# Spreading the attention's second scores over the partitions: a DRAM scratch in place of TensorE's transposes

## The chip, the cores and the metric

The kernel runs on one core of one Trainium2 chip, in float32 throughout. The metric is the device time of one execution in microseconds. Before the change it is 2218.47 us, the median of three runs (2218.12 to 2219.33).

The engines are named as in the profile: PE is TensorE's matmuls and PEld its weight loads, DVE is VectorE, ACT is ScalarE, POOL is GpSimd, and SP is SyncE, which here only issues DMAs.

## The reference

The input x has 128 graphs of 128 nodes with 512 features; `adj` is one 128 x 128 weighted adjacency matrix. Four graph layers follow each other, each added to its input and normalised over the features. What matters here is layer 2, a graph attention:

```python
h  = jnp.einsum('bnc,cf->bnf', x, W)
s1 = jnp.einsum('bnf,f->bn', h, a1)
s2 = jnp.einsum('bnf,f->bn', h, a2)
e = jax.nn.leaky_relu(s1[:, :, None] + s2[:, None, :], negative_slope=ALPHA)
e = e * mask[None, :, :]            # mask is adj
att = jax.nn.softmax(e, axis=2)
h_prime = jnp.einsum('bij,bjf->bif', att, h)
return jax.nn.elu(h_prime + beta * h)
```

For every graph, `e[i, j]` is a sum of a score of node i and a score of node j. With node i on the partitions, `s1` is one number per partition, while `s2` has to lie along the free dimension, the same row on all 128 partitions. The scores, however, come out with the node on the partitions, both of them. Turning `s2` from a column into a row on every partition is the "spread".

## The kernel before, in words

The 128 graphs go through in 32 groups of four (`G = 4`, `NG = 32`). All pieces of work of all layers and groups are put in one list, each with a due time, and the list is sorted by these times at the end (lines 817 to 827). `TABLE` (line 231) has the due times of one group, in slots of 2.48 us by the source's own constant; group g's are shifted by 28 g. So in one period of 28 slots TensorE works on layer 0 of group g+2, layer 1 of group g+1 and layers 2 and 3 of groups g and g-1, interleaved. The first two groups and the last three have due times of their own (`FIRST`, `LAST`). `InOrder` (line 18) keeps each engine's instructions, and SyncE's DMAs, in the order in which they are issued: an engine that waits holds up everything behind it on that engine. The semaphores are put in by the framework, from what each instruction reads and writes.

The names that matter:

- The large products (`product`, line 339: `y` of layer 0, `m` and `v` of layer 1, `z` of layer 2) use seven block products instead of eight (Strassen's scheme in Winograd's form). GpSimd makes the sums of the left factors (`left_factors`, line 294: tiles `s_y`, `yT` and the like). TensorE takes seven steps in the order 1, 2, 6, 5, 7, 3, 4, each of eight matmuls of 256 columns, into PSUM regions `r...`. After each step ScalarE or VectorE reads the region out (`out`, line 359). Steps 6, 7 and 4 add onto the region of step 1, so each of them has to wait until the step before it on that region has been read. For y the read is VectorE's `x<-r_y,x`, which adds to x in place.
- `scale_dots` (line 580) finishes the scores of a group on VectorE: a tile `d12`, kept as `s12[g]`, of 128 partitions x (s1, s2) x 4 graphs. Its last instruction is `d<-d,rstd`.
- `spread` (line 623) turns `s2` with four 128 x 128 transposes on TensorE, against the identity, into one PSUM bank `p_s2`, printed as `p_s` in the profile. Banks come from a ring of three (`bank`, line 82).
- `leaky` (line 632) is VectorE's `e<-p_s,d`, which adds the two scores for four graphs at once, and `e<-e`, the leaky ReLU. After it come `weighted` (GpSimd times `adj`), `greatest` (VectorE, `nm`), `exps` (ScalarE), `divide` (VectorE's `rs`, GpSimd's product), `turn_att` (four transposes, `p_eT`), and `gather`.
- SyncE's queue holds, in one period: the 16 moves of `xT` for g+1, four stores, the load of x for g+3 (1 MB, due 64 in g's slots), and the 16 moves of `relT` for g+1.

Of the kernel before, what the change touches and what calls it, by code (L numbers as in the profile page):

```python
# [8 lines left out]
FP = mybir.dt.float32  # L9
# [20 lines left out]
def kernel(  # L30
# [33 lines left out]
    pe, dve, act, pool = (InOrder(tc, e) for e in (nc.tensor, nc.vector, nc.scalar, nc.gpsimd))  # L64
    sync = InOrder(tc, nc.sync)
    B, N, D = x.shape
    P = 128
# [4 lines left out]
    G = 4  # L72
    NG = B // G
# [4 lines left out]
    work = ctx.enter_context(tc.tile_pool(name="work", bufs=1))  # L78
    small = ctx.enter_context(tc.tile_pool(name="small", bufs=4))
    psum = ctx.enter_context(tc.tile_pool(name="psum", bufs=1, space=bass.MemoryType.PSUM))  # L80

    def bank(name):
        return psum.tile([P, D], FP, tag="ps", name=name, bufs=3)
# [40 lines left out]
    ident = const.tile([P, P], FP)  # L124
# [102 lines left out]
    def row(at, step, n=G):  # L227
        return [at + i * step for i in range(n)]
# [8 lines left out]
        move_rel=row(41.2, 0.1), inverse=[42.5], v=row(42, 1, 7), attend=row(50.6, 1),  # L237
        residual=row(51.0, 1), dots=[51.7, 53.8, 54.9, 55.6], norm1=[54.6], scale=[57.2],
        apply1=row(65.4, 0.33),
        spread=[61.6], leaky=[62.0], weighted=[63.4], greatest=[64.3], exps=[64.4],  # L240
        divide=[65.8], turn_att=[68.6], with_beta=[69.0], gather=row(71.5, 1),
        z_sums=row(75.3, 0.5), z_w=row(77, 1, 7), exp=[87.5, 88.5, 90.4, 92.0],
        elu=[87.8, 89.4, 92.8, 93.8], norm2=[95.0], apply2=row(95.7, 0.33),
# [14 lines left out]
            greatest=[10.5], exps=[11.2], divide=[13.6], turn_att=[18.3], with_beta=[18.9],  # L258
# [11 lines left out]
            greatest=[52.4], exps=row(53.2, 0.6), divide=row(53.9, 0.6),  # L270
# [344 lines left out]
    s12 = {}  # L615
# [3 lines left out]

    def layer2(g, t):  # L620
        s = {}

        def spread():
            s["p"] = bank(f"p_s2_{g}")
            for b in range(G):
                pe.transpose(
                    s["p"][:, b * P : (b + 1) * P],
                    s12[g][:, 1, b : b + 1].to_broadcast([P, P]),
                    ident,
                )  # L630

        def leaky():
            e = work.tile([P, G, P], FP, tag="e", name=f"e_{g}")
            dve.tensor_tensor(
                e,
                s["p"].rearrange("p (b n) -> p b n", b=G),
                s12[g][:, 0, :, None].to_broadcast([P, G, P]),
                ALU.add,
            )
            dve.scalar_tensor_tensor(e, e, ALPHA, e, op0=ALU.mult, op1=ALU.max)  # L640
            s["e"] = e
# [89 lines left out]

        n = G // len(t["exps"])
        emit(t["spread"][0], spread)
        emit(t["leaky"][0], leaky)
        emit(t["weighted"][0], weighted)
        emit(t["greatest"][0], greatest)
# [86 lines left out]
    for g in range(NG):  # L823
        for layer in (layer0, layer1, layer2, layer3):
            layer(g, times(g))
# [31 lines left out]
```

## Time and profile before

| From the page | before |
|---|---|
| time of the runs, median | 2218.47 us |
| profiled span | 2214.6 us |
| PE busy | 2170.9 us, 98% |
| PEld busy | 1839.6 us, 83% |
| DVE busy | 1547.9 us, 70% |
| ACT busy | 1102.5 us, 50% |
| POOL busy | 907.7 us, 41% |
| DMA | 115.15 MB, mean 52 GB/s |

A line of a group in the profile gives the source line, the engine, the operation, "tile written <- tiles read", the shapes, the count, and then times. Since all operations go through one helper, every line number is L26, and one reads by tile names. Buffer numbers and group numbers are left out of the names. A timeline line gives the start and the length in us, and in brackets the idle time of that engine ahead of it with what ended it. Matmuls are pipelined: the length of a line of PE reaches to the modelled end of its last matmul, so the cost of a stretch is read from the start of one line to the start of the next.

A busy engine of 98% isn't proof that only this engine counts. Whether a change elsewhere reaches it is read from how long before the wait's end the other engines had been done.

### The profile page before, as it was taken

What the parts mean: (1) busy time and instruction counts of PE and PEld (TensorE: products, weight loads), DVE (VectorE), ACT (ScalarE), POOL (GpSimd) and SP (SyncE); (2) the same over time, 40 slices, a digit from 0 to 9 for tenths busy, and PEclk for the clock granted to TensorE, in tenths of its full rate; (3) what the DMA queues carried; (4) which work ended last, traced back from release to release, by engine and by line L of the source; (5) the groups of instructions that cost most, each with busy time, mean ns of one, the idle gap of its engine ahead of it and who ended that gap; (6) DMA issues with size and microseconds to landing.
All of it is one profiled execution on the core that took longest, in us unless ns stands there. A gap on an engine that the chain in (4) does not pass through costs nothing.

```text
span 2214.6 us, 31863 instructions
## 1 busy us (share of the span) xinstructions
PE 2170.9 (98%) x11073; PEld 1839.6 (83%) x11073; DVE 1547.9 (70%) x3290; ACT 1102.5 (50%) x2446; POOL 907.7 (41%) x743
## 2 busy tenths in 40 slices
PE   7999999999999999999999999999999999999996
PEld 5788888888888888888888888888888888888873
DVE  4657766767766767776767776767767677667676
ACT  2224445554445554445554445554455554455547
POOL 3334444334444344443344443344443344443321
PEclk9999999999999999999999999999999999999998
DMA  4011222211222211222112222112222112221101
GB/s 167 25 20 29 61 60 62 62 20 49 60 60 63 58 21 52 59 61 62 44 31 56 58 62 63 41 30 59 58 62 63 29 39 62 59 63 44 21 28 57
DMA packets 333295, 115.15 MB, mean 52 GB/s; under 512 B 297424, under 2 KB 297552, under 8 KB 333136
## 3 DMA queue, kind: packets, MB, share of 16 engines
q1 hardware_dynamic: 331936, 110.77, 19.7%
q10 hardware_dynamic: 1200, 2.36, 0.3%
q8 instruction: 88, 1.44, 0.3%
q14 instruction: 71, 0.58, 0.1%
HBM read 39.65 MB, written 33.55 MB: 33 GB/s over the span
## 4 chain that ended last, share of the span: by engine, by line
PE 93%; DVE 3%; ACT 2%; POOL 1%; issue 1%; DMA 0%; ACTq 0%; DVEq 0%; POOLq 0%
PE r_y L26 17%; PE r_v L26 17%; PE r_m L26 17%; PE r_z L26 17%; PE p_z L26 5%; PE p_rel L26 5%; PE p_y L26 5%; PE p_o L26 5%; PE p_a L26 5%; DVE x L26 1%; ACT x L26 1%; DVE st L26 1%; PE p_eT L26 1%; PE p_m L26 1%; PE p_s L26 1%
## 5 line engine op out<-in xcount | busy, mean ns | idle before, releaser
L26 ACT ACTIVATE x<-x,nmean,rstd 128x512 f32<-128x512 f32 x384 | 288.6, 808 | 120.8 <-DVE nmean L26 120.8
L26 DVE BATCH_NORM_STATS2 st<-x 128x6 f32<-128x512 f32 x384 | 263.8, 687 | 8.8
L26 POOL TENSOR_TENSOR x<-x,bias_sb 128x512 f32<-128x512 f32 x128 | 170.1, 1331 | 137.9 <-PE p_y L26 137.5
L26 DVE SCALAR_TENSOR_TENSOR x<-m,x 128x512 f32<-128x512 f32 x128 | 114.4, 894 | 108.5 <-ACT m L26 98.5
L26 POOL TENSOR_TENSOR s_x<-xT 128x512 f32<-128x512 f32 x64 | 82.2, 1285 | 261.1 <-DMA xT<-xB 250.2
L26 ACT COPY c<-r_z 128x512 f32<-128x512 f32 x124 | 71.2, 574 | 223.3 <-PE r_z L26 198.0
L26 ACT COPY yT<-p_y 128x512 f32<-128x512 f32 x128 | 75.1, 586 | 213.6 <-PE p_y L26 213.6
L26 POOL TENSOR_TENSOR rstd<-ve,mhalf 128x4 f32<-128x4 f32 (+1 forms) x99 | 98.5, 995 | 194.1 <-DVE ve L26 188.9
L26 DVE TENSOR_TENSOR x<-r_y,x 128x512 f32<-128x512 f32 x224 | 151.7, 678 | 31.2 <-PE r_y L26 31.0
L26 DVE SCALAR_TENSOR_TENSOR scr<-x,wa 128x512 f32<-128x512 f32 x256 | 161.5, 675 | 0.0
L26 DVE STREAM_TRANSPOSE xB<-x 128x512 f32<-128x512 f32 x120 | 81.2, 696 | 108.7 <-ACT x L26 97.7
L26 PEld LDWEIGHTS p_y<-adjT,x 128*128 128x128 f32 x1024 | 136.9, 196 | 11.2 <-ACT adjT L26 4.8
L26 POOL TENSOR_TENSOR s_z<-zT 128x512 f32<-128x512 f32 x31 | 39.4, 1270 | 255.9 <-ACT zT L26 255.9
L26 PE MATMUL p_y<-adjT,x 128*128 128x128 f32 x1024 | 137.6, 280 | 4.5 <-ACT adjT L26 4.5
L26 PEld LDWEIGHTS p_z<-eT,x 128*128 128x128 f32 x1024 | 134.0, 192 | 7.9 <-issue 1.0
L26 PEld LDWEIGHTS p_rel<-xT,tT 128*128 128x128 f32 x1024 | 134.1, 191 | 7.4 <-DVE tT L26 0.8
L26 DVE TENSOR_REDUCE mx<-p_a 128x1 f32<-128x512 f32 x128 | 88.3, 691 | 69.6 <-PE p_a L26 69.6
L26 PE MATMUL p_a<-x,adjT 128*128 128x512 f32 x256 | 130.8, 596 | 5.8 <-DVE mx L26 4.4
L26 ACT COPY tT<-r_m 128x512 f32<-128x512 f32 x128 | 75.6, 590 | 121.6 <-PE r_m L26 121.6
L26 PE MATMUL p_rel<-xT,tT 128*128 128x128 f32 x1024 | 134.9, 275 | 0.6 <-DVE tT L26 0.6
L26 PE MATMUL p_z<-eT,x 128*128 128x128 f32 x1024 | 134.7, 275 | 0.1
L26 PE MATMUL p_o<-v,relT 128*128 128x512 f32 x256 | 130.4, 593 | 0.3 <-ACT v L26 0.3
(129 smaller groups left out, 5268.6 us busy)
## 6 DMA issues: line engine op xcount, KB each, us to landing
out_dram<-x SPq DMA_DIRECT2D x128, 256.0 KB, 2.5
x<-in_x_dram SPq DMA_DIRECT2D x31, 1024.0 KB, 5.3
xT<-xB SPq DMA_DIRECT2D x480, 64.0 KB, 2.3
relT<-relB SPq DMA_DIRECT2D x512, 16.0 KB, 1.8
w_sb<-in_L_gnn_weight_dram ACTq DMA_DIRECT2D x1, 1024.0 KB, 5.6
x<-in_x_dram SPq DMA_DIRECT2D x4, 256.0 KB, 7.8
wq_sb<-in_L_gnn_Wq_dram SPq DMA_DIRECT2D x1, 1024.0 KB, 12.3
wk_sb<-in_L_gnn_Wk_dram SPq DMA_DIRECT2D x1, 1024.0 KB, 15.1
```

The costliest lines, as they stand in the source:

```text
L26: return lambda *args, **kw: self.tc.keep_in_program_order(op(*args, **kw))
```

## The change

For all groups but the last two, `spread` no longer uses TensorE. The s2 part of `s12[g]` (128 partitions x 4 numbers) is written by a DMA into a scratch in DRAM, which lies there as 512 numbers in a row, node by node with the four graphs side by side. A second DMA reads these 2 KB back for each of the 128 partitions, as a tile `wide` in SBUF. `leaky` reads this tile in the order graph, node, so that neighbouring elements of what it reads lie four numbers (16 bytes) apart. The piece is due at 57.3 instead of 61.6, right behind `scale_dots` (57.2), while `leaky` stays at 62.0. The last two groups have the transposes as before. It is meant to take work off TensorE.

```diff
+    dram = ctx.enter_context(tc.tile_pool(name="dram", bufs=2, space=bass.MemoryType.DRAM))
...
-        spread=[61.6], leaky=[62.0], weighted=[63.4], greatest=[64.3], exps=[64.4],
+        spread=[57.3], leaky=[62.0], weighted=[63.4], greatest=[64.3], exps=[64.4],
...
     def layer2(g, t):
         s = {}
+        late = g >= NG - 2
+
 
         def spread():
-            s["p"] = bank(f"p_s2_{g}")
-            for b in range(G):
-                pe.transpose(
-                    s["p"][:, b * P : (b + 1) * P],
-                    s12[g][:, 1, b : b + 1].to_broadcast([P, P]),
-                    ident,
-                )
+            if late:
+                p = bank(f"p_s2_{g}")
+                for b in range(G):
+                    pe.transpose(
+                        p[:, b * P : (b + 1) * P],
+                        s12[g][:, 1, b : b + 1].to_broadcast([P, P]),
+                        ident,
+                    )
+                s["s2"] = p.rearrange("p (b n) -> p b n", b=G)
+            else:
+                line = dram.tile([P, G], FP, tag="s2", name=f"s2d_{g}")
+                sync.dma_start(line, s12[g][:, 1, :])
+                wide = work.tile([P, P, G], FP, tag="s2", name=f"s2_{g}")
+                sync.dma_start(
+                    wide.rearrange("p n b -> p (n b)"),
+                    line.rearrange("n b -> (n b)")[None, :].to_broadcast([P, P * G]),
+                )
+                s["s2"] = wide.rearrange("p n b -> p b n")
 
         def leaky():
             e = work.tile([P, G, P], FP, tag="e", name=f"e_{g}")
             dve.tensor_tensor(
                 e,
-                s["p"].rearrange("p (b n) -> p b n", b=G),
+                s["s2"],
                 s12[g][:, 0, :, None].to_broadcast([P, G, P]),
                 ALU.add,
             )
```

## The prediction

> **What bounds the kernel.** I read the page first: its busy times and its chain that ended last.
>
> ```profile
> PE 2170.9 (98%) x11073; PEld 1839.6 (83%) x11073; DVE 1547.9 (70%) x3290; ACT 1102.5 (50%) x2446; POOL 907.7 (41%) x743
> PE 93%; DVE 3%; ACT 2%; POOL 1%; issue 1%; DMA 0%; ACTq 0%; DVEq 0%; POOLq 0%
> ```
>
> TensorE (PE) is the bound nearly everywhere; from 112 to 2116 us it is busy 2001.9 of 2004 us. What TensorE no longer does is gained, unless another engine then makes it wait. So I next took the view of the tile `p_s`, which the change removes, its counts being 32 groups x 4.
>
> ```profile
> L26 PE MATMUL p_s<-ident,d x128: 272/273/273, 120.1 to 2163.6; 128*128 128x128 f32 x128
> L26 DVE TENSOR_TENSOR e<-p_s,d x32: 675/681/692, 125.5 to 2164.1; 128x512 f32<-128x512 f32 x32
> ```
>
> The reader, `e<-p_s,d`, takes 675 to 692 ns in every group. Last, the timeline of one group in the middle (start, length; all groups from 1 to 29 but group 11 repeat it within 0.03 us):
>
> ```profile
> 911.24 0.17 DVE L26 TENSOR_TENSOR d<-d,rstd 128x8 f32<-128x8 f32 x1
> ...
> 920.15 1.60 POOL L26 TENSOR_TENSOR s_y<-s_y,yT 128x512 f32<-128x512 f32 x1
> 920.57 0.57 PEld L26 LDWEIGHTS p_s<-ident,d 128*128 128x128 f32 x4
> 920.78 0.60 PE L26 MATMUL p_s<-ident,d 128*128 128x128 f32 x4
> 921.08 1.22 DVE L26 SCALAR_TENSOR_TENSOR x<-m,x 128x512 f32<-128x512 f32 x1 [0.46 <-DVE x L26]
> ...
> 921.22 1.89 PE L26 MATMUL r_m<-xT,t_m 128*128 128x256 f32 x8
> ...
> 923.39 1.27 POOL L26 TENSOR_TENSOR s_y<-yT,s_y 128x512 f32<-128x512 f32 x1
> ...
> 923.74 0.68 DVE L26 TENSOR_TENSOR e<-p_s,d 128x512 f32<-128x512 f32 x1
> 924.45 0.76 DVE L26 SCALAR_TENSOR_TENSOR e<-e 128x512 f32<-128x512 f32 x1
> ...
> 935.69 0.69 DVE L26 TENSOR_TENSOR x<-r_y,x 128x512 f32<-128x512 f32 x1
> ...
> 937.32 1.89 PE L26 MATMUL r_y<-t,yT 128*128 128x256 f32 x8
> ```
>
> See three things. Matmuls overlap, so the four transposes cost not 0.60 us but the 0.44 us from 920.78 to 921.22. The reader starts while GpSimd (POOL) is in `s_y<-yT,s_y`, and isn't slowed. And the last step of the y product (937.32) accumulates into a PSUM region that VectorE (DVE) finishes reading only at 936.38: 0.94 us before.
>
> [...] `x<-m,x`, with two SBUF inputs, has a median of 693 ns but a maximum of 1574, and above it took 1.22 us beside GpSimd's 920.15 to 921.75, ending 0.55 after it; the PSUM reader `e<-p_s,d` never varies. [...] No row here reads with a 16-byte step[...]. [...]
>
> **The change part by part.**
>
> *Removed: the transposes.* 0.44 us x 30 groups = 13.2 us of TensorE's own time, all on the path. One PSUM bank request fewer out of 17 a group makes the three-bank ring no tighter.
>
> *Added: two DMAs on SyncE's queue.* The write starts when `d<-d,rstd` ends, 911.24 + 0.17 = 911.41; the reader's turn comes at 923.74, 12.3 us later. Lower bound by the nearest rows: issue 0.4 to 0.7 us each; the 16 KB `relT` moves land in 1.8 us, the 256 KB stores in 2.5; together about 0.5 + 1.8 + 0.5 + 2.5 = 5.3 us. Upper bound: 2.6 (`adj_sb`) for the write and 7.9 us for the same 256 KB broadcast of `bias_sb` in the crowded start, with issues 11.6 us. I take 6; both ends fit in, so the cost is nothing, hidden by the 12.3 us of VectorE's other work. The queue's own wait for the first landing holds up what is queued behind: the 1 MB load of x for group g+3, which was issued at 905.40 and now goes at about 914.5. It lands 5.3 us later, near 920; its first reader, `p_y` of g+3, comes one period after 908.58, at 975.4. The moves of `relT` begin at 937.97. So nobody waits. The new buffers were last used a group (DRAM: two groups) earlier.
>
> *Moved: the reader's source, from PSUM to SBUF with a 16-byte step.* Here lies the cost. First, it now has two SBUF inputs[...]. `x<-m,x` ended 0.55 us after its blocker, so the reader ends at 924.66 + 0.56 = 925.22 instead of 924.42. The next operation, `e<-e`, then runs unblocked in 0.69 and not 0.76, ending at 925.94 instead of 925.21: late by 0.73 us. Second, the stride[...]. Call the lateness L = 0.73 + 0.54 = 1.27 us[...].
>
> *Who waits for that.* VectorE works in order and the timeline shows no idle time on it that L would not also push. The chain is `e<-e`, GpSimd's masking, `nm`, the y additions, `rs`, GpSimd's `e<-e,rs` and `rstd`, `nmean`, and `x<-r_y,x` at 935.69. It ends at 936.38 + L. TensorE, 0.44 us earlier after the removed transposes, wants its last y step at 936.88. A restart costs it about 0.16: in group 0 it started 0.06 us after VectorE's `tT` ended at 125.55, and its eight matmuls then held it 1.83 us (125.61 to 127.44) instead of 1.73. So it stands still for 936.38 + L + 0.16 - 936.88 = L - 0.34. The other y steps have more room (the second: L - 0.88) and their stalls are contained in this one. Nothing of VectorE's lateness is left after it, since the next addition waits for TensorE anyhow; the following group starts afresh.
>
> *Sum.* Each group: -0.44 + (1.27 - 0.34) = +0.49 us; 30 groups: +14.7. 2218.47 + 14.7 = 2233.2, taken as 2233 us. The groups 0 and 11, where VectorE already is 0.6 to 0.8 us late, may differ, by some 1 us in all.
>
> **The rivals.**
>
> *The lock without the stride cost.* Four float32 words may be close enough. L = 0.73: -0.44 + 0.39 = -0.05 a group, -1.5 us, 2217. For it: no row here shows a stride cost.[...]
>
> *No lock: the full gain, or most of it.* If the reader isn't blocked, because a broadcast second operand doesn't count or since it slips ahead, [...] I put it at 2208. For it: TensorE is busy at 98%, and waits nowhere in these groups now. Against: `d<-d,rstd`, with a broadcast second input, took 1.12 us once (at 110.47) where its median is 0.17.
>
> *The scratch arrives late.* Were the landings to take, say, 15 us rather than 6, the reader waits, and past some 13 us each further microsecond goes through the same chain into TensorE: 30 us per microsecond, so 2260 to 2300. Against: even the crowded start's landings fit.
>
> **How the numbers follow.** Lock and stride 0.62[...]; lock alone 0.13; no lock 0.18; late scratch 0.07. Faster by over 0.2% means under 2214.0: the no-lock case mostly and a little of the lock alone, 0.20. Within 0.2%, to 2222.9: the rest of these two, 0.12. Slower: 0.68. The range 2209 to 2245 leaves out the lower half of the no-lock case (0.09), the late scratch (0.07) and a few hundredths.
>
> **What will show it.** `p_s` x8 left; the period from group to group near 67.3 us and not 66.81; the reader in the SBUF form at 1.9 to 2.1 us by its recorded start, or near 1.2 where it isn't blocked; new TensorE waits of up to 0.9 us on VectorE's `x`, ahead of the last y step, 28 to 30 times; no wait of VectorE for a DMA. If the reader takes 0.7 us beside a busy GpSimd, the lock step is wrong. If it is late by 1.3 us and TensorE still doesn't wait, the chain is. If VectorE waits for the scratch, the DMA step is.

## The result and the profile after

The kernel after takes 2227.91 us (median of four runs, 2225.93 to 2228.79), the kernel before beside it 2218.9 (2218.12 to 2219.41). The ratio is 1.004, with a 95% interval of 1.0022 to 1.0057: slower, by about 9 us. Forecast were 2233 us in a range of 2209 to 2245.

The page of the kernel after, busy times and chain that ended last:

```profile
PE 2180.0 (98%) x10953; PEld 1835.7 (83%) x10953; DVE 1572.4 (71%) x3290; ACT 1099.1 (49%) x2446; POOL 907.5 (41%) x743
PE 93%; DVE 3%; ACT 2%; POOL 1%; issue 1%; DMA 0%; ACTq 0%; DVEq 0%; POOLq 0%
```

TensorE has 120 matmuls fewer (10953 for 11073) and yet 9 us more busy time, and what the span has beyond it is the same, 44.0 us for 43.7: time in which it waits is booked as busy here, so this line can't show the new waits. VectorE is busy 24.5 us longer. The chain's shares by engine are unchanged to the per cent.

The view of the tile `p_s` of the kernel after (only the last two groups have it), and then the view of the tile `s`, the scratch's copy in SBUF:

```profile
L26 PE MATMUL p_s<-ident,d x8: 272/273/273, 2125.0 to 2172.2; 128*128 128x128 f32 x8
```

```profile
L26 DVE TENSOR_TENSOR e<-s,d x30: 1054/1785/1796, 126.4 to 2067.9; 128x512 f32<-128x512 f32 x30
```

The reader has become 1785 ns in the median (min/median/max of one) where it was 681. Its minimum, 1054, is in group 0, and group 11 has 1.07 us: the two groups where GpSimd runs nothing when the reader starts. The timeline shows a middle group, the same one as shown of the kernel before:

```profile
916.26 0.17 DVE L26 TENSOR_TENSOR d<-d,rstd 128x8 f32<-128x8 f32 x1
...
916.45 0.33 SPq L26 DMA_DIRECT2D s2d<-d  x1
...
918.39 0.33 SPq L26 DMA_DIRECT2D s<-s2d  x1
918.77 0.43 SPq L26 DMA_DIRECT2D x<-in_x_dram  x1
...
927.46 1.27 POOL L26 TENSOR_TENSOR s_y<-yT,s_y 128x512 f32<-128x512 f32 x1
927.81 1.78 DVE L26 TENSOR_TENSOR e<-s,d 128x512 f32<-128x512 f32 x1
929.62 0.69 DVE L26 SCALAR_TENSOR_TENSOR e<-e 128x512 f32<-128x512 f32 x1
...
930.40 1.27 POOL L26 TENSOR_TENSOR e<-e,adj_sb 128x512 f32<-128x512 f32 x1 [1.66 <-DVE e L26]
931.70 0.69 DVE L26 TENSOR_REDUCE nm<-e 128x4 f32<-128x512 f32 x1 [0.78 <-POOL e L26]
...
940.78 0.69 DVE L26 TENSOR_TENSOR x<-r_y,x 128x512 f32<-128x512 f32 x1
...
941.53 1.59 PEld L26 LDWEIGHTS r_y<-t,yT 128*128 128x128 f32 x8 [0.28 <-DVE x L26]
```

The reader starts at 927.81 inside GpSimd's 927.46 to 928.73 and ends at 929.59: this longer run beside GpSimd is what "the lock" stands for here. From its start to the end of `e<-e` it is now 2.50 us; before it was 1.47 (923.74 to 925.21). That is the lateness L = 1.03. The last line is the new wait: TensorE restarts 0.06 us after VectorE's `x<-r_y,x` ends at 941.47. The view of the waits has it as a row that the kernel before does not have (total us, times, longest):

```profile
PEld r_y L26 <- DVE x L26: 8.3, 29, 0.6
```

The distance from group to group (the median over starts of `p_eT`) says it most sharply, since the start of a run varies by up to some 4 us from execution to execution: 66.81 us before, 67.07 after, so +0.26 a group and +7.8 us in 30 groups. The 1 us that is left of the 9 is less than that scatter. Below, "period" means this distance.

### The profile page after: what moved, and what is told of

It reads as the page before. It is cut to its first block, busy times and chain, and to the rows that moved or that the text cites. A ratio compares the mean times of both kernels' runs of the same rounds, so it can differ in the third digit from the quotient of the medians.

```text
span 2224.0 us, 31714 instructions
## 1 busy us (share of the span) xinstructions
PE 2180.0 (98%) x10953; PEld 1835.7 (83%) x10953; DVE 1572.4 (71%) x3290; ACT 1099.1 (49%) x2446; POOL 907.5 (41%) x743
## 4 chain that ended last, share of the span: by engine, by line
PE 93%; DVE 3%; ACT 2%; POOL 1%; issue 1%; DMA 0%; ACTq 0%; DVEq 0%; POOLq 0%
PE r_y L26 18%; PE r_v L26 17%; PE r_m L26 17%; PE r_z L26 16%; PE p_z L26 5%; PE p_rel L26 5%; PE p_y L26 5%; PE p_o L26 5%; PE p_a L26 5%; DVE x L26 1%; ACT x L26 1%; DVE st L26 1%; PE p_m L26 1%; PE p_eT L26 1%; DMA bias_sb<-in_L_gnn_bias_dram 0%
```

## The experiments

All edits are against the kernel after, unless they say otherwise. Times are medians, with the ratio to the kernel before on the same chip.

**Is the time TensorE's own, or its wait for VectorE?** The transposes are put back, into a bank that nobody reads, at their old due time; the scores still come from the scratch.

```diff
+        def idle_turns():
+            if not late:
+                p = bank(f"p_s2_{g}")
+                ...                       # the four transposes of before
+        emit(28.0 * g + 61.6, idle_turns)
```

> The changed kernel, and beside the scratch TensorE also does the four transposes of before for all groups, at their old due time; nothing reads them. My theory (the end is set by the chain through VectorE, late by L = 1.03 us as the profile of the changed kernel shows): TensorE's extra 0.44 us a group lie inside its wait, the wait ahead of the last y step gets shorter by as much, and the time stays that of the changed kernel, 2228 us (2225 to 2230). Rival (the 13.2 us of the transposes were gained in full, and some 22 us were lost elsewhere, to the DMAs or to the order): 2228 + 13 = 2241 us.

Measured: 2228.35 us, 1.0042 [1.0027, 1.0057], period 67.08, which is that of the kernel after. Its waits:

```profile
PEld r_y L26 <- DVE x L26: 7.1, 29, 0.5
```

Putting 0.44 us a group, 13.2 us in all, back on TensorE costs nothing: the period stays, and its busy time is 2182.4 us, only 2.4 more than in the kernel after. The transposes fill time in which TensorE otherwise stood waiting and was booked as busy. By the prediction's chain VectorE may be 0.34 us late before the last y step loses time (the "room"), and with the transposes in place 0.34 + 0.44 = 0.78. The lateness of 1.03 exceeds both, so the chain gives the same period either way: 66.81 + 1.03 - 0.78 = 67.06 with them, 66.37 + 1.03 - 0.34 = 67.06 without. At this lateness VectorE sets the end, and the removed transposes are worth nothing.

**Do the DMAs cost anything?** The reader gets a constant tile of the same layout, and the scratch is left out.

```diff
+    still = const.tile([P, P, G], FP)
...
-                line = dram.tile([P, G], FP, tag="s2", name=f"s2d_{g}")
-                ...                       # both DMAs
+                s["s2"] = still.rearrange("p n b -> p b n")
```

> The changed kernel without the two DMAs: the reader takes a constant SBUF tile of the same shape in the same 16-byte step (left out: the second scores, which are zero in all groups but the last two). My theory (the DMAs cost nothing): 2228 us (2226 to 2230), the reader still 1.78 us by its recorded start. Rival (the cost comes with the DMAs: their traffic, the queue's wait, the load of x that now goes 9 us later): the gain shows, 2206 to 2215 us.

Measured: 2227.43 us, 1.004 [1.0025, 1.0055], period 67.07, reader 1791 ns. Nothing changes without the DMAs, so they are hidden.

**What are the transposes worth when the reader is cheap?** The reader takes a contiguous PSUM source (`wa`, whatever it holds), again without DMAs.

```diff
+                s["s2"] = wa[:, 0, :].rearrange("p (b n) -> p b n", b=G)
```

> The changed kernel with no spread at all in the first 30 groups: the reader takes a PSUM tile that is there all the time (left out: the second scores; the row of a weight stands in for them). It measures what taking the transposes away is worth by itself. My theory: 30 x 0.44 = 13.2 us, 2205 us (2203 to 2208), the reader at 0.68 us. Rival (TensorE doesn't set the time, or the matmuls around the transposes close the gap only partly): 2212 to 2219 us.

Measured: 2207.78 us, 0.9952 [0.9937, 0.9966], period 66.37. That is 66.81 - 0.44 to the hundredth. (The time itself moved by 9.9 us, from 2217.69; its interval, 7.5 to 14 us, holds the 13.2 that the period gives.) The tile `e`:

```profile
L26 DVE TENSOR_TENSOR e<-wa,d x30: 676/681/682, 128.2 to 2052.0; 128x512 f32<-128x512 f32 x30
```

**The lock or the stride?** The scratch and its 16-byte step stay, and the other operand moves to PSUM, so that only one input lies in SBUF.

```diff
-                s12[g][:, 0, :, None].to_broadcast([P, G, P]),
+                (s12[g][:, 0, :, None] if late else wa[:, 0, 0:G, None]).to_broadcast([P, G, P]),
```

> The changed kernel with scratch and 16-byte step, but the reader's second input, the first scores, comes from PSUM (left out: the first scores in the first 30 groups; values of a weight stand in). So the reader has one SBUF input. My theory[...]: the reader isn't blocked and takes 1.05 us by the stride alone, L = 0.30, no wait of TensorE, 2205 to 2207 us. Rival (the stride is the whole cost, and with it the reader is slow whatever GpSimd does): 2228 us.

Measured: 2208.57 us, 0.9956 [0.994, 0.9973], period 66.37. Its timeline:

```profile
920.63 1.28 POOL L26 TENSOR_TENSOR s_y<-yT,s_y 128x512 f32<-128x512 f32 x1
920.98 1.08 DVE L26 TENSOR_TENSOR e<-s,wa 128x512 f32<-128x512 f32 x1
922.09 0.69 DVE L26 SCALAR_TENSOR_TENSOR e<-e 128x512 f32<-128x512 f32 x1
```

Beside the same GpSimd instruction, started at the same point in it, the strided reader takes 1.08 and not 1.78 us. So the blocking comes here with the second SBUF input, even where that is a broadcast of four numbers, and the stride is the difference of 1085 to 681 ns. From the reader's start to the end of `e<-e` it is now 922.78 - 920.98 = 1.80 us, where it was 1.47 before the change. So with the stride alone L is 0.33, just under the room of 0.34, and the period shows no wait. The time is 1.6 us above the expected 2205 to 2207, less than the scatter of the start.

**Can the stride be taken out by the DMA?** The scratch is written graph by graph, so that the reader is contiguous.

```diff
+                line = dram.tile([G, P], FP, tag="s2", name=f"s2d_{g}")
+                sync.dma_start(line.rearrange("b n -> n b"), s12[g][:, 1, :])
+                wide = work.tile([P, G, P], FP, tag="s2", name=f"s2_{g}")
```

> The changed kernel with the scratch laid out graph by graph (the write goes in pieces of 4 bytes), so that the reader reads contiguous elements of SBUF; it still has two SBUF inputs. My theory: the stride's 0.37 us go, the block by GpSimd stays, the reader is 1.42 us by its recorded start, L = 0.73, the wait of TensorE 0.39 us a group, -0.05 in all: 2217 us (2215 to 2220). Rival (the stride is the whole cost): 2205 us. Rival (the block alone costs as much as both): 2228 us.

Measured: 2260.1 us, 1.0186 [1.0171, 1.0201], period 68.19. This missed. The view of the DMA issues (the last number is the median from issue to landing), first of the kernel after, then of this one:

```profile
s<-s2d SPq DMA_DIRECT2D x30, 256.0 KB, 5.4
s2d<-d SPq DMA_DIRECT2D x30, 2.0 KB, 1.4
```

```profile
s2d<-d SPq DMA_DIRECT2D x30, 2.0 KB, 8.4
```

The same 2 KB in 512 pieces of 4 bytes, not in 128 of 16, take 8.4 us to land. The timeline of a group shows the rest: the reader's turn comes at 943.0, 11.7 us after the write's issue, and that no longer suffices.

```profile
931.31 0.38 SPq L26 DMA_DIRECT2D s2d<-d  x1
...
940.90 0.33 SPq L26 DMA_DIRECT2D s<-s2d  x1
...
944.91 0.69 DVE L26 TENSOR_TENSOR e<-s,d 128x512 f32<-128x512 f32 x1 [1.91 <-DMA s<-s2d]
```

The reader waits about 2 us (59.7 us in 29 times in the view of the waits), and then runs unblocked in 0.69, because by then GpSimd is done. This is the rival of the late scratch. A wait of 59.7 / 29 = 2.06 us, with a reader no slower than before, gives 66.37 + 2.06 - 0.34 = 68.09 by the prediction's chain, near the measured 68.19.

**Does a later `nm` give VectorE room?** In the timeline after, `nm` waits 0.78 us for GpSimd's masking, with the second y addition queued behind it. Its due time is moved from 64.3 to 64.75, `exps` to 64.76, so that this addition goes first. Three kernels have this order: the contiguous one, the kernel after, and the kernel before as a control.

```diff
-        ... greatest=[64.3], exps=[64.4],
+        ... greatest=[64.75], exps=[64.76],
```

> As the contiguous scratch, and VectorE's maximum (nm) is put behind the next y addition instead of ahead of it, which takes the 0.78 us for which VectorE waits for GpSimd's masking out of the chain. My theory: L falls from 0.73 to 0.14 where the chain goes on, TensorE doesn't wait, the full gain shows: 2205 us (2203 to 2208). Rival (something other than the lateness of this chain holds TensorE, so that the order doesn't matter): as the contiguous scratch alone, 2217 us.

> The changed kernel as it is, and only the maximum is put behind the next y addition. My theory: L is 1.03 at the second y step (TensorE waits 0.15 us there) and 0.43 further on (0.09 us at the last step): -0.44 + 0.15 = -0.29 us a group, 2210 us (2207 to 2213). Rival (the order doesn't matter): 2228 us.

> The kernel before, with the transposes, and only the maximum put behind the next y addition: a control. My theory: TensorE waits for none of these operations in the kernel before, so nothing changes, 2218.5 us (2217 to 2220). Rival (the new order is worth something by itself, and what the two runs with it gain is not the end of a wait that the change brought): 2205 to 2212 us.

Measured: 2244.89 us, 1.012 [1.0105, 1.0135], period 67.65, for the contiguous one, which misses its 2205 because its scratch is still late (60.5 us in 30 waits); 2214.54, 0.998 [0.9973, 0.9987], 66.59 for the kernel after with this order, 1.5 us above its expected range; 2219.22, 1.0002 [0.9993, 1.0011], 66.81 for the control. The order alone is worth nothing in the kernel before, where no y step waits for VectorE, and 13 to 15 us where one does. So this part of the loss does sit in the y additions' lateness.

Where TensorE loses the time is seen in the starts of the seven y steps, counted from the first, in us (medians over the groups in the middle):

| Kernel | 3rd | 4th | 5th | 6th | 7th | next product |
|---|---|---|---|---|---|---|
| reader from PSUM, no transposes | 4.34 | 6.96 | 9.58 | 12.20 | 14.37 | 16.10 |
| after | 4.49 | 7.18 | 9.80 | 12.52 | 14.96 | 16.79 |
| after, with the later `nm` | 4.49 | 7.19 | 9.81 | 12.43 | 14.59 | 16.32 |

The kernel after loses 0.22 us at the third step and behind it (the expectation's "second y step", the first that has to wait for an addition), 0.10 at the sixth, and 0.37 at the seventh and behind it: 0.69 in all. With the later `nm` only the first 0.22 is left. Expected was 0.15 there; it is the start of the third step that is 0.15 late, and its eight matmuls lose 0.07 more. The view of the waits of this kernel has no row of a y step waiting for VectorE's `x` at all, so a missing row is no proof that TensorE doesn't wait; the period and the starts of the steps are.

**Can the reader be moved out of GpSimd's way?** The reader is due 63.75, behind the first y addition, when `s_y<-yT,s_y` is over.

```diff
-        spread=[57.3], leaky=[62.0], weighted=[63.4], greatest=[64.3], exps=[64.4],
+        spread=[57.3], leaky=[63.75], weighted=[63.76], greatest=[64.85], exps=[64.86],
```

> The changed kernel, computing everything, with the reader moved on VectorE: it and the leaky ReLU come behind the first y addition instead of ahead of it[...], and the maximum behind the next residual piece. My theory: the reader is no longer blocked (1.05 us), the first y addition isn't held up at all, the further ones by at most 0.3 us, TensorE waits nowhere: a period of 66.37 us and 2206 to 2209 us, as when the transposes are just left out. It would beat the kernel before by 0.4 to 0.5 per cent. Rival (the stride's 0.37 us, or the later maximum, reach TensorE all the same): the period above 66.5 us, 2212 to 2219 us.

Measured: 2224.45 us, 1.0027 [1.0016, 1.0037], period 66.93. A miss by 0.56 a group, and slower than its rival too. Its timeline:

```profile
926.30 3.62 PE L26 MATMUL r_y<-w_sb,yT 128*128 128x256 f32 x16
...
927.18 1.27 POOL L26 TENSOR_TENSOR s_y<-yT,s_y 128x512 f32<-128x512 f32 x1
...
928.28 0.69 DVE L26 TENSOR_TENSOR x<-r_y,x 128x512 f32<-128x512 f32 x1 [0.67 <-issue]
928.89 1.06 DVE L26 TENSOR_TENSOR e<-s,d 128x512 f32<-128x512 f32 x1
...
930.75 1.27 POOL L26 TENSOR_TENSOR e<-e,adj_sb 128x512 f32<-128x512 f32 x1 [2.30 <-DVE e L26]
931.19 1.38 DVE L26 SCALAR_TENSOR_TENSOR x<-c,x 128x512 f32<-128x512 f32 x1
```

The reader is unblocked, at 1.06 us. But VectorE stands idle for 0.67 us ahead of the first addition. The profile names nothing that it waits for ("issue"); since the addition starts 0.09 us after the modelled end of TensorE's first y step (926.30 + 1.89 = 928.19), it most likely waits for that. And the masking, later than before, now blocks another instruction with two SBUF inputs, `x<-c,x` (1.38 instead of 0.68). The lock is moved, not removed. The sum fits: 0.38 for the reader, -0.07 for `e<-e`, 0.67, 0.70, and -0.78 for the wait of `nm`, which is gone, make L = 0.90, and 0.90 - 0.34 is the 0.56 of the miss. The parts weren't tested singly.

**The lock alone, and an 8-byte step.** Both have a constant tile and no DMAs: one contiguous, one with every second number.

```diff
+    still = const.tile([P, G, P], FP)        # the other: [P, G, P, 2]
+                s["s2"] = still              # the other: still[:, :, :, 0]
```

> The block by GpSimd alone: the reader takes a constant SBUF tile, contiguous, no DMAs, no transposes (left out: the second scores, zero in the first 30 groups). My theory: L = 0.73 us, TensorE waits 0.39 us a group, which eats all but 0.05 us of the 0.44: a period of 66.76 us, 2216 to 2220 us, the reader 1.42 us by its recorded start. Rival (only the stride matters): a period of 66.37, 2207 us. Rival (the block alone costs as much as with the stride): 67.07, 2228 us.

> The changed kernel without the DMAs, reading a constant SBUF tile in steps of 8 bytes instead of 16 (left out: the second scores, zero in the first 30 groups). My theory (what costs is that neighbouring elements aren't adjacent, whatever the step): the reader takes 1.05 us in group 0, where GpSimd is idle, and 1.78 in the others; a period of 67.07 us. Rival[...]: 0.68 us in group 0, 1.42 in the others, a period of 66.76 us.

Measured: 2219.06 us, 1.0002 [0.9994, 1.001], period 66.75 for the contiguous one; 2219.41 in one run, period 66.76, with the 8-byte step. The tile `still` in the two, contiguous first:

```profile
L26 DVE TENSOR_TENSOR e<-still,d x30: 676/1472/1480, 128.5 to 2061.0; 128x512 f32<-128x512 f32 x30
```

```profile
L26 DVE TENSOR_TENSOR e<-still,d x30: 673/1473/1478, 128.1 to 2062.4; 128x512 f32<-128x512 f32 x30
```

The lock lengthens a contiguous reader from 676 to 1472 ns, by 0.80. The 8-byte step is free, blocked or not (1473 and 673 ns), where I had expected it to cost what the 16-byte step does.

**The version that follows from these.** The graphs are put side by side in pairs, so the reader's step is 8 bytes and the write has 256 pieces of 8 bytes; and `nm` is late. It computes everything.

```diff
+                line = dram.tile([2, P, 2], FP, tag="s2", name=f"s2d_{g}")
+                sync.dma_start(line.rearrange("h n b -> n h b"),
+                               s12[g][:, 1, :].rearrange("p (h b) -> p h b", b=2))
+                wide = work.tile([P, 2, P, 2], FP, tag="s2", name=f"s2_{g}")
...
+                s["s2"] = wide.rearrange("p h n b -> p h b n")
...
+        ... greatest=[64.75], exps=[64.76],
```

> The changed kernel, computing everything, with two edits that the runs so far point to. The scratch is laid out in two halves of two graphs, so that the write goes in 8-byte pieces and the reader's step is 8 bytes, which costs nothing in the run with a constant tile; and the maximum comes behind the next y addition. My theory: the write lands in about 3.7 us (1.4 for 128 pieces, 8.4 for 512, so about halfway by their number), the scratch is there in time, L = 0.73 us up to the second y step and 0.14 after it, TensorE waits nowhere: a period of 66.37 us and 2206 to 2210 us, 0.4 to 0.5 per cent faster than before and faster than the changed kernel by 18 to 22 us. Rival (the 256 pieces land too late, or four-dimensional access costs VectorE time): VectorE waits for the scratch or the reader takes over 1.5 us, a period of 66.6 us or more.

Measured: 2206.91 us (2206.31 to 2208.02), 0.9947 [0.9934, 0.9961], period 66.37: 12 us under the kernel before, 21 under the kernel after. Its DMA issues and its timeline:

```profile
s<-s2d SPq DMA_DIRECT2D x30, 256.0 KB, 5.5
s2d<-d SPq DMA_DIRECT2D x30, 2.0 KB, 3.0
```

```profile
922.86 1.27 POOL L26 TENSOR_TENSOR s_y<-yT,s_y 128x512 f32<-128x512 f32 x1
...
923.20 1.47 DVE L26 TENSOR_TENSOR e<-s,d 128x512 f32<-128x512 f32 x1
...
925.32 1.48 DVE L26 TENSOR_TENSOR x<-r_y,x 128x512 f32<-128x512 f32 x2
926.79 0.69 DVE L26 TENSOR_REDUCE nm<-e 128x4 f32<-128x512 f32 x1
```

The write lands soon enough (3.0 us) and VectorE never waits for the scratch. The reader is still blocked, but with two y additions ahead of `nm` the lateness is used up: TensorE's y steps start at the same distances as with the reader from PSUM (first row of the table above), and the period is the same 66.37. The whole 0.44 us of the transposes is gained. The layout in pairs was not run with the old place of `nm`; the constant tile with an 8-byte step, at 66.76, says that it would gain next to nothing there.

## Why the prediction came out right, and where a size was off

- **The transposes, 0.44 us a group.** Right to the hundredth where nothing masks it (period 66.37 with a cheap reader). In the kernel after the gain is eaten by the wait: with the transposes put back the period is the same, 67.08. (The ring of banks serves 19 requests a group in the kernel before, not the 17 that I counted: four each for `p_y`, `p_o`, `p_z` and `p_a`, one each for `p_rel`, `p_s` and `p_eT`. Nothing rests on it.)
- **The DMAs cost nothing.** Right. I took 6 us in all. In the timeline after, the write is issued at 916.45, the read 1.94 later (the queue waits for the write 30 times, 44.6 us in all) and lands 5.4 after that, near 923.8, and the reader comes at 927.81. The load of x queued behind was issued 2.3 us after `d` (918.77), lands later too (7.7 us from issue), and nobody waits for it. The scratch's removal changed the period by nothing.
- **The lock, 0.73 us of lateness.** Right in size, and in what it comes with. A contiguous reader with two SBUF inputs is 0.80 us longer beside GpSimd (1472 ns for 676); `e<-e` then runs in 0.69 and not 0.76; that leaves 0.73. With the lock alone the prediction's chain gives 66.81 - 0.44 + 0.73 - 0.34 = 66.76, and 66.75 was measured. With one input moved to PSUM the lock is gone (1085 ns beside GpSimd, 1052 free of it). By what means GpSimd holds the reader up was not shown.
- **The stride, 0.54 us: the term that was off.** The 0.54 was my estimate, and nothing in the trace before showed it. Free of the lock the 16-byte step costs 1.054 - 0.681 = 0.37 us. Behind the lock it costs only 1.785 - 1.472 = 0.31, so the two terms add up to a little less than their sum. L is therefore 0.73 + 0.31 = 1.04 (1.03 in the timeline) and not 1.27.
- **The chain into TensorE, L - 0.34.** Right. With the measured L it gives 66.37 + 1.03 - 0.34 = 67.06, and the period is 67.07; the forecast of 67.3 was high by the 0.23 us of the stride, times 30 that is 7 us. The chain holds at four other values of L: 0.33 gives no wait (one SBUF input, 66.37), 0.73 gives 66.76 (the lock alone, 66.75), 0.90 gives 66.93 (the reader moved, 66.93), and about 2.06 gives 68.09 (the late scratch, 68.19). The restart price of 0.16 is seen again at the last step: 0.06 from the end at 941.47 to 941.53, and 0.10 more in the eight matmuls behind it. One detail differs. Part of the stall, 0.32 of 0.69, falls already at the earlier y steps, so that the wait in the trace is 0.28 in most groups and 0.6 at the longest, not up to 0.9. The total stays, since VectorE's lateness at the last step sets it.
- **The rivals.** The lock without a stride cost (2217) is what the constant contiguous tile gives, 2219.06; the full gain without a lock (2208) is what one SBUF input gives, 2208.57; the late scratch (2260 to 2300) is what 4-byte pieces give, 2260.1. Each cost was thus seen by itself, and the kernel after is the case of lock and stride together.

What stays open: why a restart at the third y step loses 0.07 us more than one at the last; and that 512 pieces of 4 bytes take six times as long to land as 128 of 16 was only measured, not explained.

## What to carry to other kernels

When work is taken off the engine that bounds, look at what each reader's operands become: a tile that moves from PSUM to SBUF can make its reader a two-SBUF-input operation, and such a reader took 1472 ns here beside a GpSimd instruction and 676 free of one. Compute the room of the bounding engine's next wait, here 0.34 us after the gain; lateness above it cost close to one for one in every period here. An instruction in an in-order queue that waits while ready work stands behind it, here `nm`, is a cheap place to win lateness back: moving it gained 13 us in the kernel after. Choose a scratch's layout with both ends in mind: here the larger pieces landed sooner (1.4 us in 16-byte pieces, 8.4 in 4-byte ones), the smaller step read faster (673 ns at 8 bytes, 1054 at 16), and the layout between served both.

## What the runs showed of the hardware that I had not expected

- A step of 8 bytes between float32 elements costs VectorE nothing (673 ns for 128 x 512, contiguous 676), a step of 16 bytes costs 0.37 us (1054).
- A write of 2 KB to DRAM lands in 1.4 us as 128 pieces of 16 bytes, 3.0 us as 256 of 8, and 8.4 us as 512 of 4. From the second to the third it is more than twice the time for twice the pieces.
- A second operand that is only four numbers broadcast along the row still counts as an SBUF input for the blocking: with it a contiguous reader takes 1472 ns beside GpSimd and 676 free of it; when those four numbers lie in PSUM, a reader with the 16-byte step takes 1085 beside GpSimd and 1052 free of it.
- A TensorE that waits is mostly booked as busy in these profiles: the kernel after and the last version have the same 10953 matmuls, but 2180.0 and 2161.1 us of busy time. The difference, 18.9 us, is most of the stall, 0.70 us a group or 21 us in all, of which the row of waits shows 8.3. With the later `nm` alone, 0.22 us a group is lost and no row shows it.
